# Four layers on graphs of 256 nodes: degree and mask factors move into the evacuations from PSUM, pairs of differences become one operation, and the adjacency blocks come in four transfers

## The chip, the cores and the metric

The kernel runs on one core of a Trainium2 chip. All data are float32. The metric is the device time of one execution in microseconds (us); smaller is better. Engines are named as in the profile: PE is TensorE's matmul, PEld its weight load, DVE is VectorE, ACT is ScalarE, POOL is GpSimd, and SP is the queue that issues every DMA here.

## What is computed

64 graphs, each with node features x (256 x 512) and a weighted adjacency A (256 x 256), go through four residual layers. Each layer normalises, clips at zero, and adds the result of one graph operation:

```python
h = jnp.maximum(_layernorm(x, axis=-1), 0.0)
x = x + _L0_gnn_ref(h, adj, L0_gnn_W, L0_gnn_a)   # attention, softmax over axis 1, elu
x = x + _L1_gnn_ref(h, adj, kernel, bias)         # dh * (A + I) * dh, then relu
# layer 2
t = einsum('bnm,bmf->bnf', a, x); out = relu(t @ kernel)
mask = (sum((x != 0), axis=-1, keepdims=True) > 0)
return out * mask
# layer 3
deg = sum(adj, axis=-1, keepdims=True)
agg = einsum('bij,bjf->bif', adj, x) / maximum(deg, EPS)
return relu(concatenate([x, agg], axis=2) @ W.T)
```

(The layer-norm in front of each is left out after the first line.) The degree `deg` and the mask are one number per node, that is, one per row of the output.

## The kernel before, in words

The function `tile_adj_preln_kernel` does not issue instructions directly. Each `op(engine, us, fn, reads, writes, ...)` puts one piece of work with a written duration into a `Plan`. `Plan.place` then runs a list scheduler over all 64 graphs: written durations are multiplied by the engine's `STRETCH`; a PE piece is ranked as if it became ready `SPARE` us later than it does; among pieces that can start equally early the urgent ones go first, then those with the earliest due time. A graph's due time is `APART` times its number, with a smaller step for the last `LAST` graphs. Buffers are given out in the same pass, from the counts in the dictionary `buffers`. The pieces are emitted in the order of their planned starts, so every engine's order is fixed before the kernel runs, and on the chip each engine works its own queue in that order and waits on semaphores. About five graphs are in flight at once.

All large products are done with seven multiplications instead of eight on 2 x 2 blocks (Strassen's scheme in Winograd's form). For a product of a left side A and a right side B this needs the left sums S1 to S4 and the right sums T1, T2, T3 and T4N, which are differences of blocks. `project` (products at L543) does the seven products with three PSUM banks named z, y and v. Three times ACT or DVE takes a snapshot of z before z goes on accumulating (`keep`, L582), and DVE adds y and v to the snapshots (`total`, L584).

- Layers 0 and 1 multiply with A first (`aggregate`, L474), then with the weight. `left_sums` and `more_sums` build S1 to S4: S1 and S2 on DVE (L459, L442), S3 and S4 as two POOL operations (L446).
- Layers 2 and 3 multiply with the weight first (`neighbours`), giving y = h W, and then with A (`Gathered`). `turn` transposes h in 32 x 32 blocks on DVE and finishes the transpose with 16 DMAs on SP (L621). `neighbours` takes y out of PSUM by ACT copies and DVE additions, then makes T1, T2 and T4N on DVE and T3 on POOL (all L647). Block B12 lies in a tile of its own, `y12`.
- `block_sums` makes the four sums of A's blocks on POOL (L656, L658, L662 twice).
- In layer 2 the mask is the scale of an ACT relu (`masked`, L857) which writes a temporary that DVE adds to x (L861).
- In layer 3 the reciprocal degree `rdeg` multiplies A's columns: it is turned, sent through DRAM to a row broadcast over all partitions (`along`, name `pr`: L369, L372, L375), and one DVE operation multiplies A by it (L872). The results of layer 3 are then evacuated with plain copies and additions.
- A is loaded twice per graph: `a_nat` in one transfer (L384) for the degrees, and `ab` in eight 32 KB transfers (L673), which one DVE block transpose turns into `aT` (L676).
- At the start the weights are loaded. For each of five weight matrices POOL makes T1, T2, T3 and T4N (L260), with block B12 in a temporary tile. For the first weight, logit vectors are multiplied up on PE (`logit_weights`: transposes at L302, products at L311, copies L306 and L318). The last weight is transposed on PE in 16 groups (L340) with an ACT copy each (L347). Graphs 0 and 1 take another form of layer 0: h is transposed on PE (L761), and the attention is applied last (products `po`, L779, whose moving side e is scaled on ACT at L731).

Of the kernel before, what the change touches and what calls it, by code (L numbers as in the profile page):

```python
# [25 lines left out]
LAST, LATE = 3, 0.5  # L26

STRETCH = {"DVE": 1.15, "ACT": 1.03, "POOL": 1.25, "PE": 1.0, "DMA": 1.0}
SPARE = 0.5
# [5 lines left out]
B11, B21, B22, T1, T2, T3, T4N = range(7)  # L35
# [116 lines left out]
def kernel(  # L152
# [102 lines left out]
    def weight_sums(op, n, b12):  # L255
        w = wb[n]
        key = lambda i: b12 if i is None else f"=wb{n}.{i}"
        part = lambda g, i: g[b12] if i is None else w[:, i]
        for to, i, j in ((T1, None, B11), (T2, B22, T1), (T3, B22, None), (T4N, B21, T2)):
            op("POOL", 1.28, lambda g, to=to, i=i, j=j: nc.gpsimd.tensor_tensor(  # L260
                w[:, to], part(g, i), part(g, j), ALU.subtract),
               [key(i), key(j)], [key(to)])

    def weight(n, w):

        me = Tiles(f"w{n}", 0.0)
        me.declare("b12", [P, FH, OH], tag="ex512")
        for at, i, j in ((B11, 0, 0), (None, 0, 1), (B22, 1, 1), (B21, 1, 0)):
            block = w[i * FH * P : (i + 1) * FH * P, j * OH : (j + 1) * OH].rearrange(
                "(k p) o -> p k o", p=P  # L270
            )
            me.op("DMA", 256, lambda g, at=at, block=block: nc.sync.dma_start(  # L272
                g["b12"] if at is None else wb[n][:, at], block),
                  (), ["b12" if at is None else f"=wb{n}.{at}"])
        weight_sums(me.op, n, "b12")
        if n == 0:
            logit_weights(me)

    def logit_weights(me):
# [11 lines left out]
        blocks = {(0, 0): B11, (0, 1): None, (1, 0): B21, (1, 1): B22}  # L291
        for i in range(OC):
            declare(f"pw{i}", [P, F], "ps")
            declare(f"wt{i}", [P, F], tag="aT")
            for k in range(FC):
                at = blocks[k // FH, i // (OC // 2)]
                key = "b12" if at is None else f"=wb0.{at}"

                def go(g, i=i, k=k, at=at):
                    block = g["b12"] if at is None else wb[0][:, at]  # L300
                    o = i % (OC // 2) * P
                    nc.tensor.transpose(  # L302
                        g[f"pw{i}"][:, k * P : (k + 1) * P], block[:, k % FH, o : o + P], ident)
# [17 lines left out]
    def last_weight():  # L321
# [3 lines left out]
        for n in range(2):  # L325
            declare(f"b12_{n}", [P, FH, OH], tag="ex512")
        for c in range(O // P):
# [4 lines left out]
            for n in range(2):  # L332
                for i in range(NC):
# [3 lines left out]
                    def go(g, c=c, n=n, i=i, pw=pw):  # L337
# [7 lines left out]
                    at = (B21 if i else B11) if j == 0 else (B22 if i else None)  # L345
                    key = f"b12_{n}" if at is None else f"=wb{3 + n}.{at}"
                    op("ACT", 0.38, lambda g, n=n, at=at, o=o, pw=pw: nc.scalar.copy(  # L347
                        (g[f"b12_{n}"] if at is None else wb[3 + n][:, at])[:, :, o : o + P],
                        g[pw]), [pw], [key])
        for n in range(2):  # L350
            weight_sums(op, 3 + n, f"b12_{n}")
# [4 lines left out]
    def graph(b):  # L356
# [83 lines left out]
        def more_sums(xw):  # L440
# [4 lines left out]
            for i, o in ((A22, S3), (A12, S4)):  # L445
                op("POOL", 0.85, lambda g, i=i, o=o: nc.gpsimd.tensor_tensor(  # L446
                    g[xw][:, o], g[xw][:, i], g[xw][:, S2], ALU.subtract),
                   put(i, S2), put(o), urgent=True)
# [54 lines left out]
        class Gathered:  # L503
# [3 lines left out]
            SUMS = {S1: 0, S2: 1, S3: 2, S4: 3}  # L507
# [123 lines left out]
        def neighbours(l, w):  # L631

            y, y12 = f"y{l}", f"y12{l}"
            declare(y, [P, 7, OH], tag="xw")
            declare(y12, [P, OH], tag="ex256")
            places = {(0, 0): (lambda g: g[y][:, B11], f"{y}.{B11}"),
                      (0, 1): (lambda g: g[y12], y12),
                      (1, 1): (lambda g: g[y][:, B22], f"{y}.{B22}")}
            project([Weighted(f"hw{l}", w)], f"y{l}", plain_keep, 0.38, plain_total,
                    lambda pz: op("ACT", 0.38, lambda g: nc.scalar.copy(g[y][:, B21], g[pz]),  # L640
                                  [pz], [f"{y}.{B21}"], urgent=True), places=places)
            for eng, us, to, i, j in (("DVE", 0.48, T1, None, B11), ("POOL", 0.9, T3, B22, None),
                                      ("DVE", 0.48, T2, B22, T1), ("DVE", 0.48, T4N, B21, T2)):
                name = lambda n: y12 if n is None else f"{y}.{n}"
                of = lambda g, n: g[y12] if n is None else g[y][:, n]
                on = nc.vector if eng == "DVE" else nc.gpsimd
                op(eng, us, lambda g, on=on, to=to, i=i, j=j: on.tensor_tensor(  # L647
                    g[y][:, to], of(g, i), of(g, j), ALU.subtract), [name(i), name(j)],
                   [f"{y}.{to}"], urgent=True)

        def block_sums(l, a):
# [9 lines left out]
            for at, to, i in ((2, S3, 1), (3, S4, 0)):  # L661
                op("POOL", 0.5, lambda g, at=at, i=i: nc.gpsimd.tensor_tensor(  # L662
                    g[aw][:, at], block(g, 1, i), g[aw][:, 1], ALU.subtract),
                   [a, f"{aw}.{S2}"], [f"{aw}.{to}"])
# [5 lines left out]
        for q in range(P // Q):  # L670
            rows = adj[b].rearrange("(i r) (c q j) -> q r c i j", r=Q, c=NC, j=Q)[q]
            for c in range(NC):
                op("DMA", 32, lambda g, q=q, c=c, rows=rows: nc.sync.dma_start(  # L673
                    g["ab"][q * Q : (q + 1) * Q, c, :].rearrange("r (i j) -> r i j", j=Q),
                    rows[:, c]), (), [f"ab.{q}{c}"])
        op("DVE", 0.7, lambda g: nc.vector.transpose(g["aT"], g["ab"]),  # L676
           [f"ab.{q}{c}" for q in range(P // Q) for c in range(NC)], ["aT"])
# [4 lines left out]
        for c in range(NC):  # L682
# [6 lines left out]
        op("DVE", 0.18, lambda g: nc.vector.tensor_scalar_max(g["rdeg"], g["deg"], EPS_DEG),  # L689
           ["deg.0", "deg.1"], ["rdeg"])  # L690
        op("DVE", 0.18, lambda g: nc.vector.reciprocal(g["rdeg"], g["rdeg"]), ["rdeg"], ["rdeg"])
# [162 lines left out]
        def masked(i, key, y, y_keys, to, to_keys, n, at, tag):  # L854
            v = f"v2{tag}"
            declare(v, [P, n], tag=f"ex{n}")
            op("ACT", 0.5 if n == 256 else 0.72, lambda g: nc.scalar.activation(  # L857
                g[v], y(g), AF.Relu, scale=g["mask"][:, i : i + 1]), y_keys + [f"mask.{i}"], [v],
               urgent="pz2" in y_keys)
            into_x(2, key, at, 0.43 if n == 256 else 0.69,  # L860
                   lambda g, kw: nc.vector.scalar_tensor_tensor(  # L861
                       to(g), g[v], 0.0, to(g), ALU.add, ALU.add, **kw), [v], to_keys)

        first, second, third = pieces(2)
        project([Gathered("aT", "aw2", "y2")], 2, plain_keep, 0.38, plain_total, lambda _: masked(*first, "a"))
        masked(*second, "b")
        masked(*third, "c")
        norm(3)


        along("pr", lambda g: g["rdeg"], ["rdeg", "total2.0"])
        op("DVE", 0.69, lambda g: nc.vector.tensor_tensor(  # L872
# [61 lines left out]
```

## Time and profile before

| what | value |
|---|---|
| time, median of 3 runs | 2807.49 us (2806.62 to 2808.9) |
| the profiled execution: time | 2807.72 us |
| its span, first to last instruction | 2805.9 us |
| PE records | 12871 |
| DVE, ACT, POOL busy | 2162.8 us (77%), 1745.7 us (62%), 1415.1 us (50%) |
| DMA engines, mean busy share of q1 | 31.1% |
| granted TensorE clock, mean | 0.999 |

The profile lists one execution by engine, line and operation. A group's row gives its count, its busy time, the mean duration of one, and then the idle time of that engine just before these instructions with what ended it. Each float32 matmul appears as two PE records. The ends of PE records are modelled, so the start of the next record is the better measure of what one costs. Windows split the span into stretches with the busy time of every engine and the granted TensorE clock; the timeline lists instructions by start.

### The profile page before, as it was taken

What the parts mean: (1) busy time and instruction counts of PE and PEld (TensorE: products, weight loads), DVE (VectorE), ACT (ScalarE), POOL (GpSimd) and SP (SyncE); (2) the same over time, 40 slices, a digit from 0 to 9 for tenths busy, and PEclk for the clock granted to TensorE, in tenths of its full rate; (3) what the DMA queues carried; (4) which work ended last, traced back from release to release, by engine and by line L of the source; (5) the groups of instructions that cost most, each with busy time, mean ns of one, the idle gap of its engine ahead of it and who ended that gap; (6) DMA issues with size and microseconds to landing.
All of it is one profiled execution on the core that took longest, in us unless ns stands there. A gap on an engine that the chain in (4) does not pass through costs nothing.

```text
span 2805.9 us, 45964 instructions
## 1 busy us (share of the span) xinstructions
PE 2787.2 (99%) x12871; PEld 2440.7 (87%) x12871; DVE 2162.8 (77%) x5623; ACT 1745.7 (62%) x4246; POOL 1415.1 (50%) x2653
## 2 busy tenths in 40 slices
PE   8999999999999999999999999999999999999999
PEld 5888888888888888888888888888888888888887
DVE  7887777777777777777777777777777777777775
ACT  6766665666656666666566666665666666656552
POOL 6754554545454545454445454455554545444542
PEclk9999999999999999999999999999999999999999
DMA  6233323333332333232332332333333323322222
GB/s 172 48 83 79 78 58 73 67 65 71 70 66 60 66 83 65 64 75 57 68 70 63 76 68 61 76 67 63 76 62 71 76 51 67 62 59 45 57 48 64
DMA packets 772297, 192.91 MB, mean 69 GB/s; under 512 B 703172, under 2 KB 738636, under 8 KB 772044
## 3 DMA queue, kind: packets, MB, share of 16 engines
q1 hardware_dynamic: 772044, 189.98, 31.1%
q8 instruction: 105, 1.72, 0.3%
q14 instruction: 148, 1.21, 0.2%
HBM read 89.00 MB, written 33.68 MB: 44 GB/s over the span
## 4 chain that ended last, share of the span: by engine, by line
PE 98%; DVE 1%; ACT 0%; DMA 0%; issue 0%; POOL 0%; SPq 0%; POOLq 0%; DVEq 0%; ACTq 0%
PE pz L543 31%; PE pzy L543 16%; PE pv L543 16%; PE pt L474 16%; PE pvy L543 8%; PE py L543 8%; PE pyy L543 4%; PE pwa_w L311 0%; PE po L779 0%; DMA a_rows_w<-in_L_gnn_a_dram 0%; DVE e L698 0%; DVE e L718 0%; PE pw_w L302 0%; SPq L272 0%; DVE xs L747 0%
## 5 line engine op out<-in xcount | busy, mean ns | idle before, releaser
L543 PE MATMUL pz<-wb,xw 128*128 128x256 f32 x2048 | 523.9, 379 | 2.9 <-DVE c L811 1.2
L543 PE MATMUL pzy<-wb,hw 128*128 128x256 f32 x2048 | 516.8, 379 | 0.6 <-ACT y L582 0.6
L543 PEld LDWEIGHTS pz<-wb,xw 128*128 128x128 f32 x2048 | 388.1, 190 | 58.3 <-DVE c L811 1.2
L543 PEld LDWEIGHTS pzy<-wb,hw 128*128 128x128 f32 x2048 | 389.0, 190 | 53.8 <-ACT y L582 1.0
L436 ACT ACTIVATE h<-xs,nb,rstd 128x512 f32<-128x512 f32 x512 | 391.6, 808 | 25.9 <-POOL nb L433 22.9
L582 ACT COPY c<-pz 128x256 f32<-128x256 f32 x570 | 211.3, 371 | 307.6 <-PE pz L543 267.6
L446 POOL TENSOR_TENSOR xw<-xw 128x256 f32<-128x256 f32 x256 | 214.9, 858 | 186.8 <-DVE xw L442 113.7
L415 ACT ACTIVATE h<-xs,mv 128x512 f32<-128x512 f32 x384 | 275.8, 719 | 45.0 <-POOL mv L409 28.6
L446 POOL TENSOR_TENSOR hw<-hw 128x256 f32<-128x256 f32 x256 | 202.5, 810 | 198.8 <-DVE hw L442 99.8
L582 ACT COPY y<-pzy 128x256 f32<-128x256 f32 x384 | 142.0, 370 | 214.1 <-PE pzy L543 184.5
L584 DVE TENSOR_TENSOR c<-pv,c 128x256 f32<-128x256 f32 x380 | 160.7, 423 | 138.3 <-ACT c L582 72.2
L543 PE MATMUL pvy<-wb,hw 128*128 128x256 f32 x1024 | 262.9, 379 | 0.1
L543 PE MATMUL pv<-wb,xw 128*128 128x256 f32 x1024 | 262.9, 379 | 0.0
L543 PE MATMUL pz<-wb,hw 128*128 128x256 f32 x1024 | 262.7, 379 | 0.0
L412 POOL TENSOR_SCALAR mv<-total 128x1 f32<-128x1 f32 x192 | 48.8, 254 | 422.7 <-DVE xs L747 263.5
L474 PE MATMUL pt<-ahT,h 128*128 128x256 f32 x1024 | 241.0, 379 | 0.0
L474 PE MATMUL pt<-e,h 128*128 128x256 f32 x992 | 224.4, 379 | 0.0
L474 PEld LDWEIGHTS pt<-ahT,h 128*128 128x128 f32 x1024 | 194.5, 190 | 27.0 <-issue 0.6
L543 PEld LDWEIGHTS pvy<-wb,hw 128*128 128x128 f32 x1024 | 194.5, 190 | 26.9 <-issue 0.5
L543 PEld LDWEIGHTS pz<-wb,hw 128*128 128x128 f32 x1024 | 194.6, 190 | 26.4
L543 PEld LDWEIGHTS pv<-wb,xw 128*128 128x128 f32 x1024 | 194.2, 190 | 26.3
L698 DVE SCALAR_TENSOR_TENSOR e<-h,wa 128x512 f32<-128x512 f32 x256 | 203.8, 796 | 11.8 <-ACT wa L318 3.9
(140 smaller groups left out, 5905.4 us busy)
## 6 DMA issues: line engine op xcount, KB each, us to landing
hw<-h SPq DMA_DIRECT2D x2048, 32.0 KB
xs<-in_x_dram SPq DMA_DIRECT2D x64, 512.0 KB
out_dram<-xs SPq DMA_DIRECT2D x64, 512.0 KB
ab<-in_adj_dram SPq DMA_DIRECT2D x512, 32.0 KB
a_nat<-in_adj_dram SPq DMA_DIRECT2D x64, 256.0 KB
pr<-dpr SPq DMA_DIRECT2D x64, 128.0 KB
pl<-dpl SPq DMA_DIRECT2D x61, 128.0 KB
w3n_w<-in_L_gnn_W_dram SPq DMA_DIRECT2D x4, 512.0 KB
```

What stands on the lines that cost most here:

```text
L412: op("POOL", 0.3, lambda g: nc.gpsimd.tensor_scalar(g[mv][:, 0, 0:1], g[t][:, 0:1], -1.0 / F, None, ALU.mult), [f"{t}.0"], [f"{mv}.m0"])
L415: op("ACT", 1.0, lambda g, c=c: nc.scalar.activation(g[h][:, c, :], g["xs"][:, c, :], AF.Square, bias=g[mv][:, 0, c : c + 1], accum_out=g[ ...
L436: op("ACT", 0.81, lambda g, c=c: nc.scalar.activation(g[h][:, c, :], g["xs"][:, c, :], AF.Relu, bias=g[nb][:, c : c + 1], scale=g[rs][:, c ...
L446: op("POOL", 0.85, lambda g, i=i, o=o: nc.gpsimd.tensor_tensor(g[xw][:, o], g[xw][:, i], g[xw][:, S2], ALU.subtract), put(i, S2), put(o), ...
L474: nc.tensor.matmul(g[pt][:, kk, :], lhsT=g[h][:, c, k * P : (k + 1) * P], rhs=g[moving][:, c, :], start=(c == 0), stop=(c == NC - 1),)
L543: nc.tensor.matmul(g[t], lhsT=o.left(g, left, k), rhs=o.right(g, right, k), start=start and n == 0, stop=n == len(parts) - 1, skip_group_c ...
L582: return "ACT", lambda g, to, block: nc.scalar.copy(to, block)
L584: plain_total = (0.43, lambda g, i, to, block: nc.vector.tensor_tensor(to, block, to, ALU.add))
L698: op("DVE", 0.77, lambda g, j=j, c=c: nc.vector.scalar_tensor_tensor(g["e"].rearrange("p c n -> p (c n)"), g["h0"][:, c, :], 1.0, wa[:, j, ...
```

## The change

Layer 3 no longer scales A. Its h is multiplied by the degree (clamped from below) within the normalisation's factor (`norm(3, "deg")`), y is multiplied by `rdeg` as it is taken out of PSUM, and so are the results of layer 3: relu(rdeg * (deg * h W + A (rdeg * deg * h W'))) is the same value. The row broadcast `pr` and the multiplication of A go away. In layer 2 the mask becomes the scale of the snapshots and additions, so the two temporaries of the parts that are added last go away. T1 and T3 are one operation over two neighbouring slots, as are S3 and S4, and the last two block sums of A; block B12 now lies in the slot that T4N takes later. T4N of y moves from DVE to POOL. `ab` comes in four 64 KB transfers. The planner's constants, some written durations and the buffer counts change as well.

```diff
-LAST, LATE = 3, 0.5
-STRETCH = {"DVE": 1.15, "ACT": 1.03, "POOL": 1.25, "PE": 1.0, "DMA": 1.0}
-SPARE = 0.5
+LAST, LATE = 4, 0.5
+STRETCH = {"DVE": 1.15, "ACT": 1.06, "POOL": 1.2, "PE": 1.0, "DMA": 1.0}
+SPARE = 0.15
-B11, B21, B22, T1, T2, T3, T4N = range(7)
+B11, T4N, B22, T1, T3, T2, B21 = range(7)
+B12 = T4N
...
+    def differences(op, engs, tile, key, late=()):
+        steps = ((slice(T1, T3 + 1), slice(B12, B22 + 1), slice(B11, B12 + 1), (B11, B12, B22), (T1, T3)),
+                 (T2, B22, T1, (B22, T1), (T2,)),
+                 (T4N, B21, T2, (B21, T2), (T4N,)))
+        for (eng, us), (to, i, j, reads, writes) in zip(engs, steps):
+            on = nc.vector if eng == "DVE" else nc.gpsimd
+            op(eng, us, lambda g, on=on, to=to, i=i, j=j: on.tensor_tensor(
+                tile(g)[:, to], tile(g)[:, i], tile(g)[:, j], ALU.subtract),
+               [key(n) for n in reads], [key(n) for n in writes], **dict(late))
+    def weight_sums(op, n):
+        differences(op, [("POOL", 2.5), ("POOL", 1.3), ("POOL", 1.3)],
+                    lambda g: wb[n].rearrange("p b k o -> p b (k o)"), lambda i: f"=wb{n}.{i}")
...
-            for i, o in ((A22, S3), (A12, S4)):
-                op("POOL", 0.85, lambda g, i=i, o=o: nc.gpsimd.tensor_tensor(
-                    g[xw][:, o], g[xw][:, i], g[xw][:, S2], ALU.subtract),
-                   put(i, S2), put(o), urgent=True)
+            op("POOL", 1.45, lambda g: nc.gpsimd.tensor_tensor(
+                flat(g[xw][:, S4 : S3 + 1]), flat(g[xw][:, A12 : A22 + 1 : A22 - A12]),
+                flat(g[xw][:, S2 : S2 + 1]).to_broadcast([P, 2, FH * P]), ALU.subtract),
+               put(A12, A22, S2), put(S3, S4), urgent=True)
...
+        def row_scaled(by):
+            return (
+                lambda i, j: ("ACT", lambda g, to, block: nc.scalar.activation(
+                    to, block, AF.Copy, scale=g[by][:, i : i + 1])),
+                (0.49, lambda g, i, to, block: nc.vector.scalar_tensor_tensor(
+                    to, block, g[by][:, i : i + 1], to, ALU.mult, ALU.add)),
+            )
...
-            for eng, us, to, i, j in (("DVE", 0.48, T1, None, B11), ("POOL", 0.9, T3, B22, None),
-                                      ("DVE", 0.48, T2, B22, T1), ("DVE", 0.48, T4N, B21, T2)):
...
+            keep, total = row_scaled(by) if by else (plain_keep, plain_total)
...
+            differences(op, [("DVE", 0.7), ("DVE", 0.48), ("POOL", 0.9)], lambda g: g[y],
+                        lambda i: f"{y}.{i}", dict(urgent=True))
...
         for q in range(P // Q):
-            for c in range(NC):
-                op("DMA", 32, lambda g, q=q, c=c, rows=rows: nc.sync.dma_start(
+            op("DMA", 64, lambda g, q=q: nc.sync.dma_start(
...
-        norm(3)
-        along("pr", lambda g: g["rdeg"], ["rdeg", "total2.0"])
-        op("DVE", 0.69, lambda g: nc.vector.tensor_tensor(
-            g["aT"], g["aT"], g["pr"].rearrange("p (o n) -> p o n", o=1).to_broadcast([P, NC, N]),
-            ALU.mult), ["pr", "aT"], ["aT"], urgent=True)
+        keep, total = row_scaled("mask")
+        project([Gathered("aT", "aw2", "y2")], 2, keep, 0.38, total, last2, ["mask.0", "mask.1"])
+        relu_add(2, *second)
+        relu_add(2, *third)
+        norm(3, "deg")
         turn(3)
-        neighbours(3, 4)
+        neighbours(3, 4, "rdeg")
         block_sums(3, "aT")
-        project([Weighted("hw3", 3), Gathered("aT", "aw3", "y3")], 3, plain_keep, 0.38, plain_total,
-                lambda _: relu_add(3, *pieces(3)[0]))
+        keep, total = row_scaled("rdeg")
+        project([Weighted("hw3", 3), Gathered("aT", "aw3", "y3")], 3, keep, 0.38, total, last3, ["rdeg"])
...
-        xs=7, a_nat=1, ab=1, aT=6, h=5, mva=5, xw=5, c=2, off=1, junk=1, ex256=3, ex512=2,
-        a_rows=1, a_cols=1, turned=2, row=16, pl=1, pr=1, ps=8,
+        xs=7, a_nat=1, ab=1, aT=6, h=5, mva=4, xw=5, c=3, off=1, junk=1, ex256=2, ex512=1,
+        a_rows=1, a_cols=1, turned=1, row=16, pl=1, ps=8,
```

Here `last2` and `last3` take the block of z that is never snapshot: an ACT relu with the mask or `rdeg` as scale, then a DVE addition to x.

## The prediction

> **What bounds the kernel now.** I read the page first: busy shares, then the chain that ended last.
>
> ```profile
> PE 2787.2 (99%) x12871; PEld 2440.7 (87%) x12871; DVE 2162.8 (77%) x5623; ACT 1745.7 (62%) x4246; POOL 1415.1 (50%) x2653
> PE 98%; DVE 1%; ACT 0%; DMA 0%; issue 0%; POOL 0%; SPq 0%; POOLq 0%; DVEq 0%; ACTq 0%
> ```
>
> PE is busy 99% and makes up 98% of the chain. Busy ends are modelled, so I asked for windows, the steady part first, then the ends.
>
> ```profile
> 150.00:2650.00 2500.00, 2500.00 (x11585) 2200.78 (x11584) 1945.59 (x5096) 1570.95 (x3813) 1249.66 (x2367) 1.00 0.31 67
> 40.00:50.00 10.00, 6.46 (x17) 0.83 0.80 220
> ```
>
> From 150 to 2650 us PE never stops: 2500.00 / 11585 = 0.2158 us per record, a single rate. (The second line is PE's: busy, records, clock, DMA.) So time is to be had only in the first 150 us, in the last 150, or by breaking the middle. A graph takes 100 matmuls, 200 records, 43.2 us. Dense work of the whole program: 12768 records of 256 columns x 0.2158 = 2755.7; 32 records of 512 columns (L311, L779) x 0.432 = 13.8; 70 transposes (L302, L340, L761, L246) at about 0.11 each, 7.6. Sum 2777.1. The span is 2805.9: 28.8 us are not PE work. The last matmul starts at 2800.23, leaving some 5.2 for the drain; some 10 go by 18.7 us (weights landing, half-rate matmuls); the rest is stalls that the PE timeline and ACT's show:
>
> ```profile
> 40.65 0.44 PE L340 MATMUL pw_w<-ident,w3n_w 128*128 128x128 f32 x2 [0.15 <-DVE wh L584]
> 44.48 5.39 PE L779 MATMUL po<-wh,e 128*128 128x512 f32 x8 [3.39 <-ACT wb L347]
> 49.71 3.64 PE L474 MATMUL pt<-ahT,h 128*128 128x256 f32 x16
> 58.52 1.10 PE L543 MATMUL pz<-wb,xw 128*128 128x256 f32 x4 [0.62 <-DVE c L811]
> 88.97 1.10 PE L543 MATMUL pz<-wb,xw 128*128 128x256 f32 x4 [0.55 <-POOL mv L412]
> 97.12 1.13 PE L543 MATMUL pzy<-wb,hw 128*128 128x256 f32 x4 [0.57 <-ACT y L582]
> 2737.53 0.70 PE L543 MATMUL pv<-y,aw 128*128 128x256 f32 x2 [0.54 <-DVE y L647]
> ...
> 41.56 1.51 ACT L436 ACTIVATE h<-xs,nb,rstd 128x512 f32<-128x512 f32 x2
> 43.68 0.49 ACT L731 ACTIVATE e<-e,den 128x256 f32<-128x256 f32 x1
> ```
>
> Comparing starts with dense work: about 1.9 us in graphs 0 and 1 (19.5 to 26); 3.6 before the second `po` at 44.48 (the preceding piece was done at 40.87), behind ACT, whose last scaling of e came at 43.68; then those eight records took 5.23 instead of 3.45, at a clock of 0.83: 1.8. Then 0.8 at 58.5, 0.7, 0.7 and 0.4 near 89, 97 and 98, 0.5 between 110 and 120, 0.7 at 2737. Sum 11.1 us, 0.40%: nearly all this change could gain beyond the loading. No more comes from making DVE or POOL lighter.
>
> **What the skill says.** "TensorE: Matmul & The Clock Gate", What's actually happening: after an idle window of about 3.4 us TensorE falls to half rate. The trace agrees in kind: 3.6 us idle, then 0.83 over that window. "ScalarE: Activation LUTs", What ACT_TABLE_LOAD costs: a per-partition scale operand adds about 93 ns. Here the copy at L582 takes 371 ns, the scaled relu of the same shape from PSUM (L857, v2a) 477: 106 more. "SBUF — State Buffer", Who interferes with whom: a DVE operation with two SBUF inputs contends with a POOL operation that reads SBUF. Here L446's median is 732 ns, its longest 1248; POOL prices below are such means.
>
> **The change part by part.** Everything between the ends lies beside a full PE; I price it to see that it stays there.
>
> DVE per graph: minus L872 0.701, minus the turn of `rdeg` 0.233, minus two T4N of 0.43; plus 0.27 twice for T1 with T3 at 512 elements (0.70, as L872, against 0.43); plus nine scaled additions at 0.481 (L818) instead of 0.423, 0.52; minus 0.18 for layer 2's additions to x. Sum -0.9, 58 us in all, 77% to 75%. ACT: minus v2b and v2c, 1.23; plus v3 0.48; plus ten scaled snapshots at 0.106: +0.3 per graph. POOL: S3 with S4 at 512 elements was not seen on these tiles; the nearest row, L260 on 512 elements, has 1.35 to 1.40, single cases 1.72, against 2 x 0.83. I take 1.4, four times: -1.1; bounds 1.2 and 2.0 (no merging gain, with contention). The block sums -0.28, T4N for T3 none, one product with `deg` +0.21. Sum -1.2. SP: four `ab` issues and two of `pr` fewer. An issue of `ab` runs 0.45 us in the median. A 64 KB one was not seen: between 0.45 (-1.8 per graph) and 0.9 (none); I take 0.6. Behind it wait the `hw` transfers, but SP idles for h or a buffer before them (324 and 270 us in the waits), so neither end reaches PE. Latency: y's T1 now waits for B22, and T4N takes 0.9 on POOL instead of 0.43 on DVE, about 1.2 us per layer; `pr`'s two DMAs go. Five graphs in flight hide both.
>
> For the ends I followed the new order of instructions on each engine (no times are in it) with the durations above.
>
> 1. Graphs 0 and 1, first layer. Before, z's products follow each other and wait for ACT snapshots, 0.7 and 0.75, and some 0.5 for `xw`. Now eight transposes of graph 1 stand ahead of S3's product, and z and y of graph 1 (1.9 us) ahead of A22's. Gain 1.6. Bounds 0.7 to 1.9. POOL's merged T1 with T3 delays the first normalisation by 0.6 us; it had 4 us in hand.
> 2. Second `po`. It waits for e of graph 1, at the end of a full ACT queue. The two normalisations of h that stood ahead of the last scaling (2 x 0.71 back to back) now follow it; the exponentials come later, the additions feeding the second square slightly earlier. I get its end at 42.1 instead of 44.17, `po` at 42.3, 2.2 ahead including point 1: a further 0.6. PE arrives at about 39.5 and waits 2.8, under the window above, so I let the clock stay up: another 1.8. Bounds: 0 and 2.4 for both together.
> 3. One more of the 16 weight groups is done before it: 0.2.
> 4. New wait. Next large work is the second graph's aggregate of layer 1 (the before did graph 2's attention first). It needs its h from ACT. From e's end ACT must do 16 us of work (copies 0.26 each back to back, h 0.71, squares 0.9, exponentials 0.5), plus about 2 of waits for DVE: h at 60.2. PE, through 45.8 + 11.3 of work and about 0.9 for DVE's snapshots, is there at 58.1: 2.1 lost. With that 0.9, 3.0 against about 1.0 before: -2.0. Bounds -3.5 and 0.
> 5. Then graph 2's aggregate needs a PSUM bank that ACT frees after a mask pass: -1.05. Bounds -1.5 and -0.5.
> 6. The stalls at 89, 97, 98 and 110: snapshots and their next products are farther apart in the new order; one short spot, 0.3, remains near the layer-2 sums of graph 1. Gain 2.05. Bounds 1 and 2.3.
> 7. Tail: the stall at 2737 goes; one before the last graph's last z product appears (only two products, 1.7 us, for a scaled ACT snapshot with its hops). 0.8 for 0.7. The last addition is scaled: 0.06 on the drain. -0.15. Bounds -1 and +0.7.
>
> Sum: 1.6 + 0.6 + 1.8 + 0.2 - 2.0 - 1.05 + 2.05 - 0.15 = 3.05, so 3.0 us. Profiled execution: 2807.72 - 3.0 = 2804.7; it stands 0.23 above the median, so 2804.5 against 2807.49. About 0.2%, 5.6 us, is what I call measurable; this is 0.11%.
>
> **Rivals.**
> A. The waits I place on ACT at 58 and 64 us don't occur, because ACT, which idles 2.4 us between 44 and 61 now, idles less. Points 4 and 5 give 0 instead of -3.05, point 1 and the tail their better ends (1.9 and +0.7, about 1.1 more), and some loading is regained through shorter SP queues, up to 1: 3.0 + 3.05 + 1.1 + 0.8 = 8 us, 2799.5. For it: a window of busy ACT is not proof that its late part is needed. Against: h's chain at point 4 is all ACT work.
> B. Slower. In the new order of the middle every graph has the same pattern, 43.2 us apart. Layer 2's second snapshot of z stands between two products with only two others (four matmuls, 1.73 us) between, it grows by 0.106 to 0.477, and a normalisation (0.808) stands right ahead of it on ACT. Two hops of about 0.2 leave 0.85 us. If ACT is late by more, PE stalls in every graph: 0.2 x 58 = 11.6, 2807.5 + 11.6 = 2819 (with the ends as before). It decides from 0.1 us per graph. For it: this regularity, the smaller `SPARE`. Against: ACT has 38% idle, and the order of before had spots equally short (two products for layer 3's snapshots) with no stall in 2500 us.
> C. The clock drop of point 2 remains and ACT's wait is as long: 0.6 + 1.8 lost, 2806.9. It lies within the forecast's own range.
>
> **How the numbers follow.** Forecast (with C) 0.62, A 0.25, B 0.13. The forecast's own range is 2801 to 2809 by its bounds. The range over all, 2799 to 2811, takes in A and leaves out most of B. A lies wholly beyond 5.6 us; 0.08 of the forecast's own share does too: faster 0.33, same 0.54, slower 0.13.
>
> **What would show it.** PE full from 150 to 2650 us with 11585 records or so in that window (right: B is out). The second `po` starting near 42.3, its eight records in about 3.5. A wait of PE on ACT's h near 58 and a bank wait near 64. No stalls near 90 and 97. One in the last 10 us. It is wrong if the middle shows PE waits at a step of 43 us, or if 150 us is reached with over 5 us more work done.

## The result, and the profile after

The changed kernel takes 2811.68 us in the median of 20 runs (2810.19 to 2814.92), the kernel before 2808.06 in the 20 runs beside it (2806.62 to 2809.2). The ratio is 1.0015, with a 95% interval from 1.0008 to 1.0021: 3.6 us slower, not 3.0 faster, and 0.7 us above the upper end of the range. It is within 0.2% of no change, but on the other side of it. The profiled execution took 2810.27 us, its span is 2808.5.

The page of the changed kernel, busy time by engine:

```profile
PE 2786.2 (99%) x12871; PEld 2440.7 (87%) x12871; DVE 2186.7 (78%) x5367; ACT 1780.3 (63%) x4182; POOL 1344.2 (48%) x2328
```

PE does the same work (12871 records). POOL fell by 70.9 us, close to the 77 that the price of 1.2 a graph makes. DVE was to fall by 58 us and rose by 24, with 256 instructions fewer. That is the first sign of what went wrong.

Between 150 and 2650 us PE is busy throughout but for one wait of 0.8 us at 2497, so the difference lies at the ends again. Next the windows of PE at the start: stretch, busy time (records), granted clock, DMA share, GB/s. First the kernel before, then the changed one:

```profile
20.00:30.00 10.00, 8.80 (x43) 1.00 1.03 322
30.00:40.00 10.00, 9.97 (x44) 1.00 0.59 167
```

```profile
20.00:30.00 10.00, 7.75 (x38) 1.00 1.05 379
30.00:40.00 10.00, 7.78 (x21) 0.83 0.41 123
40.00:50.00 10.00, 7.79 (x38) 1.00 0.73 172
50.00:60.00 10.00, 10.00 (x51) 1.00 0.25 53
60.00:80.00 20.00, 16.97 (x74) 1.00 0.24 39
```

From 20 to 40 us PE handles 59 records, not 87. The timeline of PE in the changed kernel shows the places (start, duration, what, then in brackets the idle time and its releaser):

```profile
18.68 1.03 PE L546 MATMUL pz<-wb,xw 128*128 128x256 f32 x4
...
22.41 1.10 PE L546 MATMUL pz<-wb,xw 128*128 128x256 f32 x4 [0.74 <-DVE xw L444]
25.57 1.97 PE L546 MATMUL pz<-wb,xw 128*128 128x256 f32 x8 [1.19 <-ACT wh L585]
32.23 2.08 PE L546 MATMUL pv<-wb,xw 128*128 128x256 f32 x4 [2.54 <-DVE wh L587]
34.09 1.73 PE L546 MATMUL pz<-wb,xw 128*128 128x256 f32 x4
36.52 1.88 PE L789 MATMUL po<-wh,e 128*128 128x512 f32 x4
47.11 3.70 PE L789 MATMUL po<-wh,e 128*128 128x512 f32 x8 [1.91 <-ACT wb L350]
64.83 3.69 PE L477 MATMUL pt<-ahT,h 128*128 128x256 f32 x16 [1.87 <-ACT h L438]
69.19 3.72 PE L477 MATMUL pt<-e,h 128*128 128x256 f32 x16 [0.68 <-ACT xw L457]
2497.52 0.67 PE L546 MATMUL pz<-y,aT 128*128 128x256 f32 x2 [0.66 <-ACT c L637]
2800.50 1.13 PE L546 MATMUL pz<-wb,hw 128*128 128x256 f32 x4 [0.56 <-ACT c L637]
```

The reader is to see three waits between the first product z (18.68) and the first `po` (36.52), and after the longest of them eight records at about half the clock: 32.23 to 35.66 is 3.43 us for what takes 1.73 elsewhere, at a granted clock of 0.52. That stretch is 17.84 us long; in the kernel before it ran from 19.80 to 32.78, 12.98 us, with the same products in it. So 4.9 us were lost where 1.6 were to be won; 1.7 of them are the low clock, the rest is waiting. Two of the three releasers are DVE operations, and ACT, named in the third, had itself been waiting for DVE. DVE's timeline in the changed kernel:

```profile
20.14 2.12 DVE L444 TENSOR_TENSOR xw<-xw 128x256 f32<-128x256 f32 x1
22.52 1.70 DVE L708 SCALAR_TENSOR_TENSOR e<-h,wa 128x512 f32<-128x512 f32 x1
24.15 1.74 DVE L708 SCALAR_TENSOR_TENSOR e<-h,wa 128x512 f32<-128x512 f32 x1
26.00 1.57 DVE L708 SCALAR_TENSOR_TENSOR e<-h,wa 128x512 f32<-128x512 f32 x1
27.50 2.83 DVE L728 SCALAR_TENSOR_TENSOR e<-off,e 128x512 f32<-128x512 f32 x1
30.36 0.69 DVE L731 TENSOR_REDUCE top<-e 128x2 f32<-128x512 f32 x1
```

And POOL's, beside it:

```profile
19.17 2.81 POOL L264 TENSOR_TENSOR wb<-wb 128x1024 f32<-128x1024 f32 x1
22.40 1.27 POOL L448 TENSOR_TENSOR xw<-xw 128x512 f32<-128x512 f32 x1 [0.43 <-DVE xw L444]
23.63 1.71 POOL L264 TENSOR_TENSOR wb<-wb 128x512 f32<-128x512 f32 x1
...
26.98 2.79 POOL L264 TENSOR_TENSOR wb<-wb 128x1024 f32<-128x1024 f32 x1
```

The sum S2 (L444) takes 0.42 us alone and 2.12 here; a logit product (L708) 0.69 alone and 1.57 to 1.74; the min (L728) 0.7 alone and 2.83. Set against POOL, each ends just after POOL's instruction does, by a little less than its own duration (0.28 us for L444, 0.56 for L728). L444 starts at 20.14, POOL's T1 with T3 runs from 19.17 to 21.98, L444 ends at 22.26. L728 starts at 27.50, POOL's next T1 with T3 runs to 29.77, L728 ends at 30.33. These five operations, 6.8 us longer together, stand ahead of the additions PE and ACT wait for.

### The profile page after: what moved, and what is told of

Its sections match the earlier page's. It is cut to its first block, busy times and chain, and to the rows that moved or that the text cites. A ratio compares the mean times of both kernels' runs of the same rounds, so it can differ in the third digit from the quotient of the medians.

```text
span 2808.5 us, 44434 instructions
## 1 busy us (share of the span) xinstructions
PE 2786.2 (99%) x12871; PEld 2440.7 (87%) x12871; DVE 2186.7 (78%) x5367; ACT 1780.3 (63%) x4182; POOL 1344.2 (48%) x2328
## 4 chain that ended last, share of the span: by engine, by line
PE 98%; DVE 0%; ACT 0%; DMA 0%; issue 0%; POOL 0%; SPq 0%; ACTq 0%; DVEq 0%; POOLq 0%
PE pz L546 31%; PE pzy L546 16%; PE pv L546 16%; PE pt L477 16%; PE pvy L546 8%; PE py L546 8%; PE pyy L546 4%; PE pwa_w L317 0%; PE po L789 0%; DVE e L708 0%; DMA a_rows_w<-in_L_gnn_a_dram 0%; ACT h L438 0%; DVE e L728 0%; ACT e L735 0%; SPq L279 0%
## 5 line engine op out<-in xcount | busy, mean ns | idle before, releaser
L546 PE MATMUL pz<-wb,xw 128*128 128x256 f32 x2048 | 517.5, 380 | 2.4 <-ACT wh L585 1.2
L546 PE MATMUL pzy<-wb,hw 128*128 128x256 f32 x2048 | 507.8, 379 | 0.0
L708 DVE SCALAR_TENSOR_TENSOR e<-h,wa 128x512 f32<-128x512 f32 x256 | 237.8, 929 | 39.1 <-PE pt L477 33.0
L833 DVE SCALAR_TENSOR_TENSOR xs<-c,xs 128x256 f32<-128x256 f32 (+1 forms) x384 | 246.8, 644 | 4.3
L448 POOL TENSOR_TENSOR xw<-xw 128x512 f32<-128x512 f32 x128 | 196.6, 1536 | 82.0 <-ACT v L866 40.6
L585 ACT COPY y<-pzy 128x256 f32<-128x256 f32 x256 | 95.4, 373 | 201.6 <-PE pzy L546 196.4
L448 POOL TENSOR_TENSOR hw<-hw 128x512 f32<-128x512 f32 x128 | 167.2, 1306 | 96.0 <-DVE deg L699 53.8
L477 PEld LDWEIGHTS pt<-e,h 128*128 128x128 f32 x992 | 188.4, 190 | 26.6 <-ACT xw L457 1.1
L425 POOL TENSOR_TENSOR rstd<-rstd,minus_half 128x2 f32<-128x2 f32 x256 | 194.4, 759 | 21.0
```

Of the source, the lines that this page charges most:

```text
L425: op("POOL", 0.72, lambda g: nc.gpsimd.tensor_tensor(g[rs], g[rs], minus_half, ALU.pow), [rs, "=half"], [rs])
L448: op("POOL", 1.45, lambda g: nc.gpsimd.tensor_tensor(flat(g[xw][:, S4 : S3 + 1]), flat(g[xw][:, A12 : A22 + 1 : A22 - A12]), flat(g[xw][:, ...
L477: nc.tensor.matmul(g[pt][:, kk, :], lhsT=g[h][:, c, k * P : (k + 1) * P], rhs=g[moving][:, c, :], start=(c == 0), stop=(c == NC - 1),)
L546: nc.tensor.matmul(g[t], lhsT=o.left(g, left, k), rhs=o.right(g, right, k), start=start and n == 0, stop=n == len(parts) - 1, skip_group_c ...
L585: return "ACT", lambda g, to, block: nc.scalar.copy(to, block)
L708: op("DVE", 0.77, lambda g, j=j, c=c: nc.vector.scalar_tensor_tensor(g["e"].rearrange("p c n -> p (c n)"), g["h0"][:, c, :], 1.0, wa[:, j, ...
```

## The experiments

Every time below is a median of 5 to 21 runs, beside the kernel before (2807.9 to 2808.4 in the five sets of runs). The changed kernel was timed in the set of the result only, so a difference to it, or between kernels of two sets, carries up to 0.5 us of that spread. Planned times are those of the planner's clock, not of the profile. "Theory A" says that POOL's weight sums stretch the DVE operations beside them; B that the planner's new constants put the instructions in a worse order; C that merged operations hold things up, since the first half is not released before the second. D, E and F arose on the way: D that sums moved elsewhere cost as much there, E on what DVE waits for (below), F that merging S3 with S4 matters, since PE waits for both where it waited for one.

**Planner's constants, and sums held back.** Three kernels let the planner order everything anew. The first holds the sums of layers 1 to 3 back (`op.ready` starts at 30.5 instead of 0); the second and third exchange the constants of the two kernels:

```diff
+HELD = [0.0, 30.5, 30.5, 30.5, 30.5]      # hold: earliest planned start, by weight
-LAST, LATE = 4, 0.5                        # oldconst; before_newconst the other way
-STRETCH = {"DVE": 1.15, "ACT": 1.06, "POOL": 1.2, "PE": 1.0, "DMA": 1.0}
-SPARE = 0.15
+LAST, LATE = 3, 0.5
+STRETCH = {"DVE": 1.15, "ACT": 1.03, "POOL": 1.25, "PE": 1.0, "DMA": 1.0}
+SPARE = 0.5
```

> The changed kernel, with POOL's weight sums of layers 1 to 3 planned no earlier than 30.5 us of the planner's clock, behind graph 1's S3 and S4. Theory A (POOL's sums run beside graph 0's and graph 1's logit products, min and max on DVE and stretch them: 0.69 to 1.6 - 2.8 us each): the four L708 between 22 and 28 us take 0.7 to 0.8, L731's maximum is done near 26 us, not 31, PE loses under 2.5 us between 20 and 36 instead of 6.7, and the time is 2807 (-4.5). Theory B (the planner's new constants put graph 1's logit products ahead of graph 0's min and max; order alone): L708 becomes shorter or not, PE's idle there stays above 5 and the time is 2810.5 to 2812. Theory C (merged operations block POOL for 2.4 to 2.8 us): only the first T1/T3 in the way of S3/S4 counts, so -1, 2810.7.

> The changed kernel with the planner's constants of the kernel before (LAST 3, ACT 1.03, POOL 1.25, SPARE 0.5). Theory A: the same POOL sums still lie beside graph 0's logit products and its min, so most of the loss stays: 2810 to 2811. Theory B: graph 0's min and max go ahead of graph 1's logit products again, PE's idle from 20 to 36 us falls to under 3 and the time to 2807 (-4.5). Theory C: no change, 2811.7.

> The kernel before with the changed kernel's planner constants (LAST 4, ACT 1.06, POOL 1.2, SPARE 0.15) and nothing else. Theory B: it takes on most of the loss, 2811. Theory A: what matters is which DVE operations lie beside POOL's sums, so it loses only if the order brings them together: 2807.5 to 2809.5. Theory C: 2808 (unchanged).

Measured: hold 2817.21, oldconst 2827.40, before_newconst 2820.02. All three are slower than the changed kernel. Constants and operations belong together: the old operations take 2808.1 with the old constants and 2820.0 with the new, the new ones 2827.4 with the old and 2811.7 with the new. Theory B, which had the old constants alone win back 4.5 us, is out; A and C missed these totals as well. In `oldconst` the longest waits of PE are 5.4 us for POOL's `rstd` near 59 us and 5.2 for ACT's e near 96; in `before_newconst` the losses are spread from 20 to 100 us, the longest 3.1. So no one place shows what a constant does.

`hold` confirms A in the first stretch and refutes its total. DVE's and POOL's timelines of hold:

```profile
22.22 1.28 DVE L712 SCALAR_TENSOR_TENSOR e<-h,wa 128x512 f32<-128x512 f32 x1
...
23.43 0.68 DVE L712 SCALAR_TENSOR_TENSOR e<-h,wa 128x512 f32<-128x512 f32 x1
...
24.84 0.69 DVE L732 SCALAR_TENSOR_TENSOR e<-off,e 128x512 f32<-128x512 f32 x1
25.56 0.69 DVE L735 TENSOR_REDUCE top<-e 128x2 f32<-128x512 f32 x1
...
38.55 2.30 DVE L761 SCALAR_TENSOR_TENSOR xs<-exa,xs 128x512 f32<-128x512 f32 x1
```

```profile
21.68 1.27 POOL L452 TENSOR_TENSOR xw<-xw 128x512 f32<-128x512 f32 x1 [1.50 <-DVE xw L448]
...
36.70 3.60 POOL L266 TENSOR_TENSOR wb<-wb 128x512 f32<-128x512 f32 x2
```

With POOL out of the way the min (here L732) takes 0.69 instead of 2.83 and the maximum is done at 26.2 instead of 31.0, as expected; PE loses 1.3 us from 20 to 40 instead of 4.5. The one stretched logit product, at 22.22, lies beside S3 and S4. But the sums now lie beside other operations (L761, 2.30 us), PE waits 2.1 us near 41 for an addition on DVE that comes behind it, and PE's mean clock is 0.67 between 40 and 50 us. More is lost from there on than was gained.

**Only POOL's order changed.** The next kernels keep every engine's order as it is and move only the weight sums within POOL's queue, so that nothing else is rearranged:

```diff
-        for op in sorted(self.ops, key=lambda op: (op.start, op.at)):
+        for op in sorted(self.ops, key=lambda op: (op.start if op.moved is None else op.moved, op.at)):
+MOVED = {(1, 0): 32.0, (1, 1): 33.0, (1, 2): 33.1, (2, 0): 46.0, (2, 1): 46.1, (2, 2): 46.2}  # late_sums
+MOVED = {(1, 0): 32.0, (1, 1): 43.9, (1, 2): 44.0, (2, 0): 54.6, (2, 1): 54.7, (2, 2): 54.8}  # late_sums2
```

(weight, step): place in the planner's time. `before_late` does the same to the kernel before.

> The changed kernel with every engine's order of instructions kept, except that POOL takes layer 1's weight sums behind graph 1's S3 and S4 and layer 2's behind graph 4's first normalisation. Theory A (POOL's sums stretch the DVE operations beside them): PE loses under 1.5 us from 20 to 36 and its clock stays up, the second po starts at 42 to 43 instead of 47.1, and the time is 2806 to 2807 (-5). Theory D (what is gained there is lost between 40 and 80 us, where the next DVE operations lie beside the postponed sums, or PE waits for wb): the first stretch is repaired all the same, but the time is 2809 or more.

> As late_sums, with layer 1's second and third sum behind graph 3's first normalisation (beside DVE's statistics, which have not been seen stretched) and layer 2's sums later still. Theory A: 2805 to 2807, and the DVE operations between 30 and 42 us at their short durations. Theory D: PE waits for layer 1's sums near 50 us (a wait of PE on wb from POOL), 2808 or more.

> The kernel before with every engine's order kept, except that POOL takes the weight sums of layers 1 and 2 later. Theory A: L718 of graph 0 (1.66 us) and one L698 of graph 1 (1.58) fall to 0.7, the second po starts up to 2 us earlier and its clock drops less or not: 2805 to 2807. Theory D: the sums meet other DVE operations later: 2808 to 2810.

Measured: late_sums 2808.26 (ratio to before 1.0002, 0.9994 to 1.0010), 3.4 below the changed kernel and between the forecasts of A and D; late_sums2 2812.87; before_late 2809.60. In late_sums the first stretch is whole (1.5 us lost from 20 to 40, clock up) and the second `po` starts at 41.26, better than expected; but its eight records run at a low clock (5.24 us). DVE and then POOL in late_sums show where the postponed sums of layer 2 went:

```profile
44.45 2.16 DVE L435 SCALAR_TENSOR_TENSOR nb<-mv,rstd 128x2 f32<-128x2 f32 x1
...
48.43 1.75 DVE L712 SCALAR_TENSOR_TENSOR e<-h,wa 128x512 f32<-128x512 f32 x1
```

```profile
44.24 2.35 POOL L266 TENSOR_TENSOR wb<-wb 128x1024 f32<-128x1024 f32 x1
```

An operation on two columns waits 2 us for a POOL instruction of 1024. So A holds, and so does D. In late_sums2 the time is within D's forecast, but the loss did not come as expected, from PE waiting for `wb`: PE waited 1.9 us for DVE's snapshot near 57, and 4.3 near 65 for something that the profile doesn't name. In `before_late` the two DVE operations fell to 0.69 us each, as A had it, but the time is D's: the kernel before wins nothing, with a new wait of 1.5 us on ACT near 38.

Why had the kernel before been spared, with POOL as busy at the same time? Its DVE and POOL timelines:

```profile
23.52 1.27 DVE L399 BATCH_NORM_STATS2 stats<-xs 128x6 f32<-128x512 f32 x2
24.92 1.66 DVE L718 SCALAR_TENSOR_TENSOR e<-off,e 128x512 f32<-128x512 f32 x1
26.62 0.69 DVE L721 TENSOR_REDUCE top<-e 128x2 f32<-128x512 f32 x1
27.22 0.42 DVE L584 TENSOR_TENSOR wh<-pv,wh 128x256 f32<-128x256 f32 x1
```

```profile
23.55 1.27 POOL L260 TENSOR_TENSOR wb<-wb 128x512 f32<-128x512 f32 x1
24.77 1.26 POOL L260 TENSOR_TENSOR wb<-wb,b_w 128x512 f32<-128x512 f32 x1
25.99 1.72 POOL L260 TENSOR_TENSOR wb<-wb 128x512 f32<-128x512 f32 x1
```

Statistics, a maximum and an addition with one side in PSUM pass beside POOL at their usual durations; in these lines only the min, with two operands in SBUF, waits (so does one logit product of graph 1, 1.58 us at 28.38). In the new order three logit products and the min, all with two SBUF operands, lie in that place.

**Merged or split, in place.** Theory E: such a DVE operation waits until the running POOL instruction ends, so merging two POOL instructions doubles the longest wait. These kernels keep all orders of the changed kernel and issue the merged operations as two, at the same place:

```diff
-            op(eng, us, lambda g, ...: on.tensor_tensor(tile(g)[:, to], ...))      # T1 with T3, shortened
+            op(eng, us, lambda g, ...: [on.tensor_tensor(tile(g)[:, to], ...)
+                                        for to, i, j in ((T1, B12, B11), (T3, B22, B12))])
```

`split_w` does it for the weights' sums alone, `split_s` for S3 with S4, `split_in_place` for both and y. `single` has the weights' four operations too, but tells the planner, which then orders everything anew.

> The changed kernel with every engine's order kept, in which T1 and T3 of the weights, of y, and S3 and S4 are issued as two operations each at the place of the merged one. Theory A: POOL's share of time beside DVE is about the same, so the first 40 us stay as they are: 2811 to 2813. Theory C (the merged operation holds things up, since its first half is not released before its second): 2809 or below. If merging relieves POOL where it matters, slower: 2814 or more.

> The changed kernel, all orders kept, with only the weights' T1 and T3 issued as two POOL operations of 512 elements in place of one of 1024. Theory E (a DVE operation with its operands in SBUF waits until the POOL instruction that is running ends, so a merged instruction doubles the longest wait): L444 of graph 0 falls from 2.12 to about 1.0 and L728 from 2.83 to 1.7, and most of split_in_place's gain is here: 2808 to 2809. Theory F (it is S3 and S4 that matter, since PE waits for both where it waited for one): 2811 to 2812.

> The changed kernel, all orders kept, with only S3 and S4 issued as two POOL operations. Theory E: the operation of 1024 elements still stands in front of graph 0's S2 and min: 2810.5 to 2812. Theory F: 2808.

> The changed kernel with the weight sums as four POOL operations of 512 elements each, as before; all else as changed. Theory A: POOL works as long beside DVE as in the changed kernel (5.1 against 4.9 us a group), so 2811 to 2812. Theory B: no change, 2811.7. Theory C: S3 and S4 of graph 0 start earlier, the stalls between 20 and 36 us shrink by 2 or more, 2809.

Measured: split_in_place 2807.46 (ratio to before 1.0001, 0.9992 to 1.0009), split_w 2808.55 (1.0002, 0.9993 to 1.0010), split_s 2811.35 (1.0012, 1.0005 to 1.0018), single 2822.21; the changed kernel has 1.0015 (1.0008 to 1.0021). For split_in_place I had expected, by theory A, no change; it won 4.2, which met C's number, and theory E came from that. C doesn't explain why DVE operations that read none of the sums become shorter; E does, and its two numbers for split_w, 1.0 and 1.7 us, were given before it ran. DVE in split_w:

```profile
20.71 1.04 DVE L445 TENSOR_TENSOR xw<-xw 128x256 f32<-128x256 f32 x1
...
26.72 1.75 DVE L729 SCALAR_TENSOR_TENSOR e<-off,e 128x512 f32<-128x512 f32 x1
```

They fell from 2.12 and 2.83 to these, and the time by 3.1 us: merging T1 with T3 of the weights, an edit that I had costed at nothing, makes most of the slowdown. Part of it comes by way of PE's clock: all 20 executions of the changed kernel have a mean clock of 0.998 or 0.999, eight of split_w's 13 have 1.000. In split_s, where the 1024-element operation stays, L444 still takes 2.12 and nothing is won. `single`, with nearly the instructions of split_w, is 13.7 us slower than it and outside all three forecasts: PE waits 5.4 us for e on ACT near 94. A kernel that the planner orders anew therefore doesn't measure the edit.

Merging S3 with S4 shows in the steady part instead, where it is hidden. The logit product's group before, after, and in split_s:

```profile
L698 DVE SCALAR_TENSOR_TENSOR e<-h,wa 128x512 f32<-128x512 f32 x256 | 203.8, 796 | 11.8 <-ACT wa L318 3.9 <-ACT h L436 3.8
```

```profile
L708 DVE SCALAR_TENSOR_TENSOR e<-h,wa 128x512 f32<-128x512 f32 x256 | 237.8, 929 | 39.1 <-PE pt L477 33.0 <-ACT wa L324 2.5 <-ACT h L438 0.9
```

```profile
L707 DVE SCALAR_TENSOR_TENSOR e<-h,wa 128x512 f32<-128x512 f32 x256 | 208.4, 814 | 36.3 <-PE pt L476 30.4 <-ACT wa L324 2.5 <-ACT h L438 0.8
```

Split, DVE is busy 2129.1 us instead of 2186.7 and POOL 1431.6 instead of 1344.2. The merge saves POOL 87 us and costs DVE 58.

**Both, and the sums farther out.**

`late_split` is late_sums and split_w together. `spread` is late_split with layer 2's sums where layer 3's stood, near 76 us, and layer 3's later; `spread_all` splits S3 and S4 too; `spread_keep1` has the weights' T1 and T3 and S3 and S4 split, and only the sums of layers 2 and 3 moved (y stays merged, so it is split_in_place but for that). `by_hand` and `spread_hand` add moves of single instructions on DVE, POOL and ACT to late_split and spread, `spread_h1` adds two to spread_all. `spread_all_again` is spread_all once more.

```diff
-MOVED = {..., (2, 0): 46.0, (2, 1): 46.1, (2, 2): 46.2}
+MOVED = {..., (2, 0): 75.85, (2, 1): 79.71, (2, 2): 81.27, (4, 0): 84.27, (4, 1): 90.75,
+         (4, 2): 94.63, (3, 0): 104.5, (3, 1): 110.0, (3, 2): 111.0}          # spread
+BY_HAND = {("ACT", ("1", "h1.1"), 2): 57.5, ("ACT", ("1", "h1.0"), 2): 57.55,  # by_hand, spread_hand
+           ("DVE", ("1", "total1.0"), 1): 50.92, ("POOL", ("3", "dh"), 1): 59.1, ...}
+BY_HAND = {("ACT", ("1", "h1.1"), 2): 59.60, ("ACT", ("1", "h1.0"), 2): 59.605}  # spread_h1
```

> late_sums with the weights' T1 and T3 split as well. Theory E: the sums now lie mostly beside operations that don't wait for POOL, so splitting adds little: 2806.5 to 2808.5. If the two gains add up, 2804 to 2805.

> late_split with a few instructions of graphs 1 to 3 between 50 and 60 us moved ahead or back, so that graph 1's layer-1 normalisation is not behind graph 2's logits on DVE, graph 3's degrees on POOL and graph 3's and 4's normalisations on ACT. If the wait of graph 1's aggregate on ACT's h (2.0 us near 61 in late_sums) is due to that order alone, it goes: 2.0 less than late_split, 2804.5 to 2806.5. If the next wait (0.67 on the bank copied at L461) grows in its place: the same as late_split.

> late_split with layer 2's weight sums not near 45 us but near 76 us, where layer 3's stood, and layer 3's later still; every engine's own order kept but for POOL's sums. If layer 2's postponed sums cause the stalls near 50 us: these go (1.6 us from 50 to 60 in late_sums, 2.4 in late_split), 2805 to 2807. If those stalls are in the order itself: 2808 to 2809.5. If POOL's sums near 76 us make the first hw of graph 0 late: stalls from 80 to 150 us appear, 2810.

> spread with the instructions of graphs 1 to 3 moved as in by_hand. If graph 1's aggregate waits on the order: 1 to 2 us less than spread. If the bank copied at L461 takes its place, as in by_hand: the same as spread within 0.5.

> spread with S3 and S4 split too. Theory E: the operations that wait for S3 and S4 wait 0.6 less each, the logit products of graph 1 among them: the same as spread or up to 1 less. If POOL's two operations (1.85 against 1.28 us) count: up to 1 more.

> split_in_place with only the sums of layers 2 and 3 moved to 76 us and later; layer 1's stay at 19 and 25 us. Theory E: one T1 and T3 less beside graph 0's min, so its maximum is done near 26 us instead of 27.9 and 2805.5 to 2807. If layer 1's sums alone do the damage: 2807.5, as split_in_place.

> spread_all once more. If its 2805.8 was its level: 2805 to 2806.5, 1.5 to 3 below the kernel before. If it was chance: as spread and split_in_place, 2806.3 to 2807.5.

> spread_all with graph 1's layer-1 normalisation (L443) ahead of graph 2's exponentials on ACT. PE's wait of 1.9 us near 58 us falls by 0.5; the time by 0.5 (2805.3), or by nothing if the aggregate of graph 2 takes it up.

| kernel | median us | ratio to before, 95% |
|---|---|---|
| late_split | 2809.24 | 1.0001 (0.9993 to 1.0010) |
| by_hand | 2809.30 | 1.0005 (0.9996 to 1.0013) |
| spread | 2806.35 | 0.9993 (0.9985 to 1.0001) |
| spread_hand | 2807.71 | 0.9999 (0.9990 to 1.0007) |
| spread_keep1 | 2808.57 | 1.0001 (0.9993 to 1.0010) |
| spread_all | 2805.84 | 0.9993 (0.9985 to 1.0002) |
| spread_all_again | 2806.29 | 0.9994 (0.9986 to 1.0002) |
| spread_h1 | 2805.83 | 0.9990 (0.9982 to 0.9998) |

The two gains (3.4 and 3.1 below the changed kernel) don't add up where late_sums put layer 2's sums (late_split is a miss, 0.7 above its bound), and mostly do when these leave 45 us: `spread` is 2.9 below late_split and 5.3 below the changed kernel. `spread_keep1` is slower than both of its expectations: with layer 1's sums beside graph 0's softmax the min still takes 1.75 us and the maximum is done at 28.4, not 26, so moving the others wins nothing that can be seen. The moves of by_hand removed the wait they aimed at, and the next one, a PSUM bank that an ACT copy frees, grew from 0.7 to 2.2 us: the alternative that I had named. spread_hand missed both of its forecasts; in its profile the clock fell twice, and none of its 13 executions has a mean clock of 1.000, against 11 of spread's 13. A fall costs about 1.7 us (3.41 us at half the clock), enough for the 1.4 by which it is slower. spread_all_again lies within its first forecast and at the edge of the second, so it is not shown that spread_all is better than spread. In spread_all PE runs step 1 as forecast (its timeline):

```profile
18.69 1.03 PE L550 MATMUL pz<-wb,xw 128*128 128x256 f32 x4
...
29.68 1.88 PE L793 MATMUL po<-wh,e 128*128 128x512 f32 x4
...
40.35 3.70 PE L793 MATMUL po<-wh,e 128*128 128x512 f32 x8 [1.96 <-ACT wb L355]
```

From the first z to the first `po` it takes 10.99 us, without a wait. `spread_h1`, the only one of the faster kernels whose interval excludes no change (barely, and as one of eight tried), is about 2.2 us faster than the kernel before and 5.9 faster than the changed one. Its own move is worth nothing that can be seen against spread_all: the wait on h fell from 1.9 to 1.4 us and the bank's grew from 0.7 to 1.2.

## Why the prediction was wrong, by its steps

Comparing starts in the profiled executions, whose spans differ by 2.6 us:

| step | forecast us | measured us |
|---|---|---|
| loading, up to the first z (not forecast) | 0 | +1.1 |
| 1, first z to first `po` | +1.6 | -4.9 |
| 2 and 3, up to the second `po` | +0.8 | +1.1 |
| 2, clock in the second `po` | +1.8 | +1.7 |
| 4 and 5, new waits near 60 to 75 us | -3.05 | about -3 |
| 6, stalls from 89 to 120 us | +2.05 | +2.3 |
| 7, tail and drain | -0.15 | -0.1 |
| a wait at 2497 (not forecast) | 0 | -0.8 |

(Plus is a gain; z 19.80 to 18.68; `po` 32.78 to 44.48 against 36.52 to 47.11; its eight records 5.23 against 3.54.)

**Step 1 failed, and it alone turned the sign.** As the prediction put it: a gain of 1.6 with bounds 0.7 and 1.9, and "POOL's merged T1 with T3 delays the first normalisation by 0.6 us; it had 4 us in hand". I followed the one chain that reads POOL's result and looked no farther: what the instruction does to other DVE work stood at nothing. The runs showed that DVE operations that read nothing of it wait for its end, five of them 6.8 us longer together. Taking POOL's sums away repaired the stretch (hold, late_sums), and splitting T1 from T3 at the same place took 3.1 us off. The forecast's order of PE was right: where the sums are elsewhere, the stretch is 2.0 us shorter than before, at the better bound (spread_all). The bounds were wrong because they varied PE's order and ACT's queue only, with DVE at the durations it has when POOL is idle.

**What would have told.** The prediction cited the Trainium skill, "SBUF — State Buffer", section "Who interferes with whom", and used it for POOL's price only. That section also states of the shared port pair: "it's an exclusive lock." Read as an exclusive lock, it means that the waiting side stands still for the rest of the other's instruction. The trace agrees: 0.42 became 2.12 us beside an instruction of 2.81 and 1.04 where that was two.

**DVE's price per graph** was -0.9, 58 us in all; measured +24. Its operations were priced right: the scaled addition took 484 ns (481 forecast), y's merged T1 with T3 688 (700). What was missed is 82 us, and waiting for POOL makes 58 of it by the merge of S3 with S4 alone (split_s). In the steady part it is hidden, as forecast. ACT rose by 0.54 us a graph (34.6 in all) instead of 0.3, of which its scaled snapshots (474 ns against 372) and relus account for 0.26 to 0.28; the rest was not traced to a line. POOL fell by 1.1 (1.2 forecast; four times 1.4 against 1.66 saves 1.04, not 1.1, so the forecast's own sum is 1.1); S3 with S4 took 1.31 to 1.54 us (1.4); an `ab` issue took 0.63 (0.6).

**Steps 2 to 6 were sized about right but started late.** The second `po` came at 47.1 instead of 42.3, by what step 1 had lost. Counted from the first z, it was forecast at 22.5 us; the changed kernel took 28.4, the kernels with layer 1's sums moved at a fixed order 21.7 to 22.4. That its clock stayed up was luck: the wait was 1.9 us, not 2.8, and waits of that length made the clock fall in other kernels (see the last section). The 0.83 that the prediction read as the clock of the second `po` before is the mean of 40 to 50 us; over those records it was 0.67. The prediction's sum of dense work is 0.4 us too high (12768 x 0.2158 is 2755.3), and nothing rests on that. **Step 7** was right for the tail; the wait at 2497, one ACT snapshot late in one graph, was overlooked.

**The rivals.** A fell: both waits occurred. B fell: but for one wait of 0.8 us the middle is full. C didn't occur at the second `po`, but the same drop came at 32 us after step 1's wait. The true slower case, POOL's sums stretching DVE, was not among them.

What stays open: how the new waits of steps 4 and 5 could be removed (each move that shortened one lengthened the next), and why the loading took 1.1 us less, which no run separates.

## What to carry to other kernels

A sum on POOL with its operands in SBUF, as in all cases here, has two costs: its own time for those who read its result, and a closed door for DVE operations with two SBUF operands until it ends. Before merging or moving POOL work, list what DVE does beside it, and which of that is critical; merge where DVE's work is from PSUM or has slack, and keep POOL's instructions short where it isn't. Where a planner orders the work, test an edit at a fixed order first: a new plan moved these kernels by 5 to 16 us, against 0 to 4 for a single edit at a fixed order.

## What was not expected of the hardware

- Beside POOL, DVE's statistics of x, a maximum and additions from PSUM kept their durations, while even an operation on two columns (L435, 0.15 us alone) took 2.16. So what counts here is not how much is read. One operation with a single SBUF operand was held as well: the comparison that makes `off` (0.41 us alone) took 0.90 in hold, to 0.29 us after the end of POOL's T1 with T3; why it and not the statistics, no run shows.
- POOL waits too, less: its 512-element sum took 1.27 us alone and 1.71 beside DVE's logit products, the 1024-element one 2.35 and 2.79.
- Whether a wait near 2 us costs clock depends on where it lies. Where the clock falls in the 20 profiled executions, it is 0.50 for 3.41 us or for two or three times that, and within one execution these stretches start whole multiples of 3.41 us apart, as on a grid. Two steps of the grid in late_sums and two in spread, PE's busy time (records) and clock; both kernels waited 1.99 us for the second `po`:

```profile
39.14:42.55 3.41, 1.42 (x5) 1.00 0.55 97
42.55:45.96 3.41, 3.41 (x5) 0.50 0.26 42
```

```profile
41.23:44.64 3.41, 1.67 (x4) 1.00 0.48 75
44.64:48.06 3.42, 3.42 (x13) 1.00 0.28 45
```

In late_sums the whole wait lies in one step, in spread 0.25 us of it in the step before. Over the 20 profiled executions, from 20 to about 130 us, a step in which PE idled 1.97 us or more was followed by a low clock in all 20 cases (three were low already), one with 1.85 to 1.93 in four of eight; below that a clock that was up fell only once (oldconst, 1.30, in a step with eight short transposes). Before the second `po`, waits of 1.76 to 1.99 us left the clock up in ten kernels (at most 1.84 us in one step), and waits of 1.80 to 1.99 made it fall in five (1.85 or more), at 1.5 to 3.0 us each. "TensorE: Matmul & The Clock Gate", What's actually happening, gives a free-running idle window of about 3.4 us. The grid agrees with that; but some 2 us of idle time in a window were enough. The grid lies differently in each execution, so one kernel does both: of spread_all's 26 executions ten have a mean clock of 1.000 (2803.4 to 2805.8 us) and 16 of 0.999 (2804.7 to 2809.6).
- In profiles of kernels whose first 20 us hold almost the same instructions, PE's second batch of transposes, which waits for the first weights, started anywhere from 5.97 us (spread_all_again) to 7.52 (spread_hand). Up to 1.5 us between two profiled executions can come from this.
